# Reordering VectorE and ScalarE steps in a two-layer graph attention kernel

## The chip, the core and the metric

The kernel runs on one core of a Trainium2 chip. The metric is the device time of one execution in microseconds. Before the change it is 2905.23 us, the median of 3 runs (2905.09 to 2909.05).

A core has five engines that the text names: TensorE (PE; its weight loads are shown apart as PEld), VectorE (DVE), ScalarE (ACT), GpSimd (POOL) and SyncE (SP). Each works through its own queue of instructions, and they wait for one another by semaphores. In this kernel SP issues nearly all transfers between HBM and the core's own memory (SBUF). PSUM is the memory that TensorE writes its products to.

## The reference

Two layers run over 64 graphs of 256 nodes with 512 features each, in float32, each layer with a residual and a layer norm:

```python
# layer 0: graph attention, 8 heads of 64
feats = einsum('bnf,hfu->bhnu', X, W)
e_self, e_neigh = einsum('bhnu,hu->bhn', feats, a_self), einsum('bhnu,hu->bhn', feats, a_neigh)
dense = leaky_relu(e_self[..., :, None] + e_neigh[..., None, :], 0.2) + -1e10 * (1 - A)
out = relu(concat(softmax(dense) @ feats) + b)
x = layernorm(x + out)
# layer 1: attention with adjacency and distance (here the adjacency again) added to the softmax
q, k, v = split(x @ W_qkv)
attn = 0.33 * softmax(mask(q @ k.T / 8)) + 0.33 * adj + 0.33 * exp(-dist)
x = layernorm(x + (attn @ v) @ W_out + b_out)
```

## The kernel before

**The loop.** One graph (b) is a unit of work. The main loop (L1469) runs over b = 1 to 63 and calls two functions in turn: attention0_beside_projections1(b) (L1266), where layer 0's attention of graph b is mixed with layer 1's projections of graph b-1, and attention1_beside_projections0(b) (L1350), where layer 1's attention of graphs b-1 and b-2 is mixed with layer 0's projection of graph b+1. So four graphs are in flight. One pass of both functions is called a turn here. start() and end() hold the first and the last graphs.

**The order is written out by hand.** do(stage, b, step, ...) (L1160) emits one step and then calls in_order() (L94), which ties every new instruction to the one before it on the same engine. So each engine runs its instructions exactly in the order in which the do lines stand, and a step that is moved past another changes the order on every engine that both use.

**Products with seven instead of eight parts.** Four big products (layer 0's projection pf, q and k pq, values pv, output po) are 2 x 2 block products in the form with seven products and some sums. left_factors (L290) makes the sums of the moving side, four VectorE differences t1 to t4: t2 reads t1, t4 reads t2, and t3 stands alone. It serves xC (from x, L442), hC (from the first layer's output, L851) and oC (from layer 1's heads, in half_blocks, L1036). seven() (L309) issues the products and their combination. Its PSUM banks matter here: p1, p6, p7 and p4 accumulate in one bank ("chain"), and after each of them ScalarE copies the bank (L329) before the next may add to it. The adds (qk_add, v_add, product_add, add: L332) are on VectorE.

**What the change touches, in the order of a turn:**
- attend1 squares (L1029) and store (L1128): layer norm of a finished graph; squares on ScalarE with small steps on GpSimd, then two activations on ScalarE (L391) and the output's transfer on SP. rows_again and load_rows issue two more transfers on SP.
- proj1 qk p1, p2, p6, p5, p7 and, later, p4, p3: q and k. "The third copy" is the copy of p6, q and k's third product; it stands behind the store's two activations in ScalarE's queue.
- proj0 columns (L579): one VectorE difference nd, then two small exponentials on ScalarE (ccol, and the factor kept in V0).
- proj0 scaled(h) (L646): 2 activations for each of 8 heads on ScalarE, 16 in all; attend0 weights(h) (L680): 2 VectorE steps for each head.
- turned xC: the four differences of x for the next graph.
- attend0 product (L702): TensorE's av, 128 matmuls; rec0 (L724): two reciprocals on VectorE; norm0 (L729): 16 activations on ScalarE that read them.
- attend1 weights(g) (L979), g = 0 to 3: a VectorE product and, on its result, a VectorE sum, 128 x 1024 each.
- proj1 values: pv, seven parts; proj0 product: pf, seven parts; aT: a VectorE transpose of the adjacency.
- softmax1 scores(g) (L872): TensorE's pz, then two exponentials on ScalarE (L896), one for each half j; both(g) (L904): a VectorE pair sum; sums (L927): TensorE's row sums pd; invert (L933): VectorE's transpose, reciprocal and product with the row mask, then a ScalarE copy; inverted (L950): VectorE's transpose and two transfers.
- proj1 hT: VectorE's transpose of hb, which SP reloads from HBM.
- shared (L472): the additive part of layer 1's attention: a VectorE sum (part 0), two VectorE steps with the mask, even (L490) and a last sum (part 1).

The lines of the output's stretch, as they stand before:

```python
do("softmax1", b - 1, "scores", 2)
do("softmax1", b - 1, "scores", 3)
do("attend1", b - 2, "half_blocks", 1)
do("softmax1", b - 1, "both", 2)
do("attend1", b - 2, "product", "p1")
```

## Time and profile before

| what | before |
|---|---|
| median of 3 runs | 2905.23 us |
| the profiled execution's own time | 2909.9 us |
| its span, first to last instruction | 2908.1 us |
| mean granted TensorE clock | 0.994 |
| HBM traffic, over the span | 123 GB/s |
| one turn in the middle (1388.55 to 1432.66 us) | 44.11 us |
| in that turn: TensorE busy, its weight loads | 44.03 us, 33.94 us |
| in that turn: VectorE, ScalarE busy | 40.31 us, 27.51 us |

How to read it: the page and the answers of the trace give the busy time of an engine as the union of its instructions, so two that overlap are counted once. A line of the timeline has the start, the length, the engine, the source line, the operation, what it writes and reads, the shape and the count; in square brackets stands how long the engine had been idle and whom it waited for. A line of the waits has the time in total, the number of times and the longest. The ends of TensorE's matmuls are modelled, so stalls of TensorE are read from starts.

### The profile page before, as it was taken

Reading aid. Unit: us, or ns where it says so; the run is one execution under the profiler, and the core shown is the slowest. Engines: PE = TensorE matmul, PEld = TensorE weight load, DVE = VectorE, ACT = ScalarE, POOL = GpSimd, SP = SyncE. Lnnn points to the kernel's source line nnn. Section 1 sums busy time; section 2 is a strip of 40 time slices with the busy share of each in tenths; the row PEclk is TensorE's granted clock in tenths of the full one; section 3 lists DMA queues with packets and bytes.
Section 4 is the critical chain, followed back from the end, with each engine's and each line's share of the span. In section 5 each row is a group of like instructions: output and inputs, shape, how many; then the busy total and the mean of one; then the engine's idle time right before and its main releaser. Section 6 shows DMA issues by size and latency. Waiting matters only on the chain.

```text
span 2908.1 us, 93475 instructions
## 1 busy us (share of the span) xinstructions
PE 2867.5 (99%) x39110; PEld 2210.9 (76%) x39110; DVE 2589.3 (89%) x5147; ACT 1761.9 (61%) x4905; POOL 234.9 (8%) x526
## 2 busy tenths in 40 slices
PE   8899999999999999999999999999999999999998
PEld 7677777877777777877877877777777778778775
DVE  6799999999989989999999999999899999998984
ACT  3556666665666666666666656656666666666663
POOL 0001000000100100000000001001000000000001
PEclk8999999999999999999999999999999999999999
DMA  6345444454454454454444554554554544544432
GB/s 136 89 126 125 128 136 119 129 141 119 124 143 118 123 135 120 129 134 121 133 121 129 139 119 129 135 124 122 135 124 127 136 115 134 133 122 134 119 111 70
DMA packets 778972, 363.89 MB, mean 125 GB/s; under 512 B 694604, under 2 KB 696636, under 8 KB 762552
## 3 DMA queue, kind: packets, MB, share of 16 engines
q1 hardware_dynamic: 776440, 357.37, 47.5%
q8 instruction: 311, 5.10, 0.8%
q14 instruction: 109, 0.89, 0.1%
q10 hardware_dynamic: 2112, 0.52, 0.1%
HBM read 289.42 MB, written 68.13 MB: 123 GB/s over the span
## 4 chain that ended last, share of the span: by engine, by line
PE 77%; ACT 8%; DMA 7%; DVE 3%; SPq 2%; issue 2%; POOL 2%; ACTq 0%; DVEq 0%; POOLq 0%
PE pq_p L87 26%; PE pv_p L87 13%; PE po_p L87 10%; PE pf_p L87 9%; PE av L714 8%; ACT p L896 4%; PE pz L881 4%; PE av L998 3%; DMA hb<-hs 3%; DMA hs<-x 2%; PE pd L916 2%; SPq L122 2%; DMA gs<-grow 1%; ACT x L391 1%; ACT junk L372 1%
## 5 line engine op out<-in xcount | busy, mean ns | idle before, releaser
L87 PE MATMUL pq_p<-hC,wqk_sb 128*64 128x128 f32 x8192 | 485.3, 274 | 4.9 <-ACT qk L329 2.9
L87 PEld LDWEIGHTS pq_p<-hC,wqk_sb 128*64 128x64 f32 x8192 | 449.4, 137 | 21.0 <-ACT qk L329 20.6
L691 DVE SCALAR_TENSOR_TENSOR pT<-gb,ccol,at 128x256 f32<-128x256 f32 x992 | 403.3, 479 | 50.3 <-ACT ccol L588 50.3
L87 PE MATMUL pq_p<-hT,wqk_sb 128*64 128x128 f32 x6144 | 358.2, 273 | 0.6 <-DVE hT L129 0.5
L87 PEld LDWEIGHTS pq_p<-hT,wqk_sb 128*64 128x64 f32 x6144 | 342.4, 137 | 10.5 <-DVE hT L129 1.0
L896 ACT ACTIVATE p<-pz,hide 128x512 f32<-128x512 f32 x512 | 315.0, 682 | 30.9 <-PE pz L881 30.5
L745 ACT ACTIVATE x<-av,rec 128x64 f32<-128x64 f32 x1008 | 224.8, 366 | 155.5 <-DVE rec L727 155.5
L988 DVE TENSOR_TENSOR p<-p,ct 128x1024 f32<-128x1024 f32 x252 | 308.8, 1225 | 8.6
L981 DVE TENSOR_TENSOR p<-p,rb 128x1024 f32<-128x1024 f32 x252 | 303.7, 1205 | 5.1 <-DMA rb<-rs 5.1
L87 PE MATMUL pv_p<-wv_sb,hC 128*64 128x256 f32 x2048 | 250.5, 386 | 9.8 <-ACT v L329 9.8
L714 PE MATMUL av<-v,pT 128*64 128x65 f32 x8192 | 255.5, 223 | 2.5 <-issue 2.0
L881 PE MATMUL pz<-qk 64*128 64x256 f32 x2048 | 256.2, 389 | 1.8 <-ACT p L896 1.7
L714 PEld LDWEIGHTS av<-v,pT 128*64 128x64 f32 x8192 | 251.5, 139 | 4.9 <-issue 4.6
L87 PE MATMUL pf_p<-wf_sb,xC 128*64 128x264 f32 x1984 | 254.0, 386 | 0.1
L648 ACT ACTIVATE v<-v 128x64 f32<-128x64 f32 x1024 | 251.8, 338 | 0.0
L87 PE MATMUL po_p<-wo_sb,oC 128*64 128x256 f32 x1984 | 238.4, 382 | 4.3 <-DVE o L332 1.0
L881 PEld LDWEIGHTS pz<-qk 64*128 64x128 f32 x2048 | 187.1, 186 | 69.4 <-issue 48.9
L998 PE MATMUL av<-p,v 128*64 128x256 f32 x2016 | 228.8, 379 | 0.2 <-DVE p L988 0.2
L329 ACT COPY v<-pv_p 128x256 f32<-128x256 f32 x256 | 102.3, 399 | 196.1 <-PE pv_p L87 195.9
L87 PEld LDWEIGHTS pv_p<-wv_sb,hC 128*64 128x64 f32 x2048 | 149.5, 138 | 90.1 <-ACT v L329 26.4
L87 PEld LDWEIGHTS po_p<-wo_sb,oC 128*64 128x64 f32 x1984 | 136.9, 137 | 95.4 <-ACT o L329 31.5
L87 PEld LDWEIGHTS pf_p<-wf_sb,xC 128*64 128x64 f32 x1984 | 148.4, 137 | 71.3 <-DVE v L332 0.8
(165 smaller groups left out, 4399.7 us busy)
## 6 DMA issues: line engine op xcount, KB each, us to landing
rb<-rs SPq DMA_DIRECT2D x63, 1024.0 KB
gb<-gs SPq DMA_DIRECT2D x62, 1028.0 KB
hs<-x SPq DMA_DIRECT2D x64, 512.0 KB
xb<-in_x_dram SPq DMA_DIRECT2D x252, 128.0 KB
x<-in_x_dram SPq DMA_DIRECT2D x63, 512.0 KB
hb<-hs SPq DMA_DIRECT2D x252, 128.0 KB
y<-hs SPq DMA_DIRECT2D x63, 512.0 KB
out_dram<-y SPq DMA_DIRECT2D x63, 512.0 KB
```

Source lines behind the costliest of these rows:

```text
L87: matmul(dst[cols], lhsT[:, cols], rhs, **flags)
L122: nc.sync.dma_start(dst[q * B : (q + 1) * B], src.rearrange("(k r) (c q s) -> q r c k s", r=B, q=Q, s=B)[q],)
L329: nc.scalar.copy(out[COPIES[p]], dst)
L648: nc.scalar.activation(V0[b][:, t, h, :U], V0[b][:, t, h, :U], AF.Copy, scale=V0[b][:, t, h, U : U + 1],)
L691: nc.vector.scalar_tensor_tensor(pT[h][:, j, :], GB[b][h], CCOL[b][:, j, h : h + 1], AT[b][:, j, :], op0=ALU.max, op1=ALU.mult,)
L714: matmul(av[r * half : (r + 1) * half, k, :], pT[h][:, j, i : i + half], V0[b][:, j, h, :UA], start=(j == 0), stop=(j == T - 1),)
L745: nc.scalar.activation(X1[b][:, t, h * U : (h + 1) * U], av[:, k, :U], AF.Copy, scale=REC0[g][:, t, k : k + 1],)
L881: matmul(pz[:, r, j, :], QK[b][rows, g, 1, j * P : (j + 1) * P], QK[b][rows, g, 0, :], start=True, stop=True,)
L896: nc.scalar.activation(p[:, :, j, :], pz[:, :, j, :], AF.Exp, bias=hide[:, j, b : b + 1], scale=U**-0.5,)
L981: nc.vector.tensor_mul(p, p, REC[b][:, k : k + 2, g // 2, :] .unsqueeze(2) .to_broadcast([P, 2, T, N]),)
L988: nc.vector.tensor_add(p, p, CT[b].unsqueeze(1).to_broadcast([P, 2, T, N]))
L998: matmul(av[0][r * U : (r + 1) * U, g % 2, :], V1[b][:, j, 2 * g + r, :], PROBS[b][g][:, r, j, :], start=(j == 0), stop=(j == T - 1),)
```

## The change

No instruction is added or taken away; steps are put in another order.
- left_factors takes the list of differences to make, and makes them as t1, t3, t2, t4 by default.
- attend1 weights(g) can be made in two steps (product, then sum), and other VectorE steps stand between the two.
- x's four differences move from ahead of attend0's product to behind the two reciprocals, between the steps of weights 0 and 1.
- columns moves ahead of the second squares; q and k's p6 moves ahead of the store, rows_again and load_rows.
- aT moves between the steps of weights 2, and add 11 between those of weights 3.
- The exponentials of scores 3 are issued apart: the first stays, the second moves behind the output's p1. hT moves ahead of the last pair sum.
- The row sums move ahead of hC, and the steps of invert alternate with hC's four differences.
- even moves from shared's second part to its first.

```diff
--- before.py
+++ after.py
@@ -287,16 +287,18 @@
     k1, k2 = slice(0, C2), slice(C2, C)
     n1, n2 = slice(0, P), slice(P, N)
 
-    def left_factors(sums, hT, part=None):
+    def left_factors(sums, hT, which=(0, 2, 1, 3)):
 
         t1, t2, t3, t4 = (sums[:, i] for i in range(4))
-        if part != 1:
-            nc.vector.tensor_sub(t1, hT[:, k1, n2], hT[:, k1, n1])
-            nc.vector.tensor_sub(t2, hT[:, k2, n2], t1)
-        if part == 0:
-            return
-        nc.vector.tensor_sub(t3, hT[:, k2, n2], hT[:, k1, n2])
-        nc.vector.tensor_sub(t4, hT[:, k2, n1], t2)
+        for i in which:
+            if i == 0:
+                nc.vector.tensor_sub(t1, hT[:, k1, n2], hT[:, k1, n1])
+            elif i == 1:
+                nc.vector.tensor_sub(t2, hT[:, k2, n2], t1)
+            elif i == 2:
+                nc.vector.tensor_sub(t3, hT[:, k2, n2], hT[:, k1, n2])
+            else:
+                nc.vector.tensor_sub(t4, hT[:, k2, n1], t2)
 
 
 
@@ -474,6 +477,10 @@
             if part != 1:
                 CT[b] = work.tile([P, T, N], FT, tag="ct", name=f"ct_{b}", bufs=3)
                 nc.vector.tensor_add(CT[b], pa, FAR[0])
+                FAR[2] = work.tile([P, N], FT, tag="far", name=f"even_{b}", bufs=1)
+                nc.vector.tensor_scalar(
+                    FAR[2], mrow, -LA / N, LA / N, op0=ALU.mult, op1=ALU.add
+                )
             if part == 0:
                 return
             for j in range(T):
@@ -485,13 +492,8 @@
                     op0=ALU.mult,
                     op1=ALU.mult,
                 )
-
-            even = work.tile([P, N], FT, tag="far", name=f"even_{b}", bufs=1)
-            nc.vector.tensor_scalar(
-                even, mrow, -LA / N, LA / N, op0=ALU.mult, op1=ALU.add
-            )
             nc.vector.tensor_add(
-                CT[b], CT[b], even.unsqueeze(1).to_broadcast([P, T, N])
+                CT[b], CT[b], FAR[2].unsqueeze(1).to_broadcast([P, T, N])
             )
 
         def from_rows():
@@ -871,8 +873,8 @@
 
         def scores(g, part=None):
 
-            if part == 1:
-                exponentials(g, PZ.pop(g), range(T))
+            if part:
+                exponentials(g, PZ[g], range(T) if part == 1 else (part - 2,))
                 return
             pz = psum.tile([P, 2, T, N], FT, tag="sc", name=f"pz_{b}_{g}", bufs=2)
             for j in range(T):
@@ -930,22 +932,27 @@
                 sums(pd, g)
             PD[0] = pd
 
-        def invert():
+        def invert(step=None):
 
             K = 2 * N // B
-            zd = work.tile([P, K, B], FT, tag="far", name=f"zd_{b}", bufs=1)
-            nc.vector.transpose(
-                zd.rearrange("p k s -> p (k s)"), PD[0].rearrange("p g n -> p (g n)")
-            )
-            inv = small.tile([P, K], FT, tag="inv", name=f"inv_{b}", bufs=2)
-            nc.vector.reciprocal(inv, zd[:, :, 0])
+            if step in (None, 0):
+                zd = PD["blocks"] = work.tile([P, K, B], FT, tag="far", name=f"zd_{b}", bufs=1)
+                nc.vector.transpose(
+                    zd.rearrange("p k s -> p (k s)"), PD[0].rearrange("p g n -> p (g n)")
+                )
+            zd = PD["blocks"]
+            if step in (None, 1):
+                inv = PD["inv"] = small.tile([P, K], FT, tag="inv", name=f"inv_{b}", bufs=2)
+                nc.vector.reciprocal(inv, zd[:, :, 0])
+            if step in (0, 1):
+                return
+            inv = PD["inv"]
             nc.vector.tensor_mul(
                 inv.rearrange("p (g i) -> p g i", g=2),
                 inv.rearrange("p (g i) -> p g i", g=2),
                 rowmask[:, b // B, :, b % B].unsqueeze(1).to_broadcast([P, 2, N // B]),
             )
             nc.scalar.copy(zd, inv.unsqueeze(2).to_broadcast([P, K, B]))
-            PD["blocks"] = zd
 
         def inverted():
             zd = PD["blocks"]
@@ -976,15 +983,18 @@
             oT = work.tile([P, C, N], FT, tag="xC", name=f"oT_{b}", bufs=1)
         av = {}
 
-        def weights(g):
+        def weights(g, step=None):
             p, k = PROBS[b][g], 2 * (g % 2)
-            nc.vector.tensor_mul(
-                p,
-                p,
-                REC[b][:, k : k + 2, g // 2, :]
-                .unsqueeze(2)
-                .to_broadcast([P, 2, T, N]),
-            )
+            if step != 1:
+                nc.vector.tensor_mul(
+                    p,
+                    p,
+                    REC[b][:, k : k + 2, g // 2, :]
+                    .unsqueeze(2)
+                    .to_broadcast([P, 2, T, N]),
+                )
+            if step == 0:
+                return
             nc.vector.tensor_add(
                 p, p, CT[b].unsqueeze(1).to_broadcast([P, 2, T, N])
             )
@@ -1035,10 +1045,10 @@
 
         def half_blocks(part):
             if part == 1:
-                left_factors(SEVEN["sums"], oT, 1)
+                left_factors(SEVEN["sums"], oT, (3,))
                 return
             SEVEN["sums"] = oC = work.tile([P, 4, C2, P], FT, tag="xC", name=f"oC_{b}", bufs=1)
-            left_factors(oC, oT, 0)
+            left_factors(oC, oT, (0, 2, 1))
             SEVEN["o"] = o = io.tile([P, T, F], FT, tag="xb", name=f"o_{b}", bufs=1)
             SEVEN["product"], SEVEN["add"] = seven_rows(
                 f"po_{b}",
@@ -1269,13 +1279,13 @@
         if b > 1:
             do("attend1", b - 4, "squares", slice(0, 1), False)
             do("proj1", b - 1, "qk", "p1")
+            do("proj0", b, "columns")
             do("attend1", b - 4, "squares", slice(1, 2), slice(0, 2))
             do("proj1", b - 1, "qk", "p2")
-            do("proj0", b, "columns")
+            do("proj1", b - 1, "qk", "p6")
             do("attend1", b - 4, "store")
             do("attend1", b - 3, "rows_again")
             load_rows(b)
-            do("proj1", b - 1, "qk", "p6")
             for h in range(HG):
                 do("proj0", b, "scaled", h)
                 do("attend0", b, "weights", h)
@@ -1287,14 +1297,18 @@
                 do("attend0", b, "weights", h)
             do("proj1", b - 1, "qk", "p7")
             do("proj1", b - 1, "qk_add", 22)
-            if b + 1 < NB:
-                do("turned", b + 1, "xC")
         for g in range(2):
             for t in range(T):
                 do("attend0", b, "product", g, t)
         do("attend0", b, "rec0", 0)
         do("attend0", b, "rec0", 1)
-        do("attend1", b - 2, "weights", 0)
+        turned = 1 < b < NB - 1
+        do("attend1", b - 2, "weights", 0, 0)
+        if turned:
+            do("turned", b + 1, "xC", (0, 2))
+        do("attend1", b - 2, "weights", 0, 1)
+        if turned:
+            do("turned", b + 1, "xC", (1,))
         if b == 1:
             do("proj0", b, "shared")
             load_rowmask()
@@ -1309,7 +1323,10 @@
             do("attend0", b, "norm0", 1, t)
         if b > 1:
             do("proj1", b - 1, "qk", "p3")
-        do("attend1", b - 2, "weights", 1)
+        do("attend1", b - 2, "weights", 1, 0)
+        if turned:
+            do("turned", b + 1, "xC", (3,))
+        do("attend1", b - 2, "weights", 1, 1)
         if b > 1:
             do("proj1", b - 1, "qk_add", 12)
         do("attend0", b, "end")
@@ -1327,13 +1344,14 @@
             load(b + 2)
         do("proj0", b + 1, "product", "p1")
         do("proj1", b - 1, "values", "p4")
-        do("attend1", b - 2, "weights", 2)
+        do("attend1", b - 2, "weights", 2, 0)
         do("attend0", b, "squares", slice(0, 1), False)
         do("proj0", b + 1, "product", "p6")
         do("attend0", b, "squares", slice(1, 2), slice(0, 2))
         do("proj1", b - 1, "values", "p3")
+        do("proj0", b + 1, "aT")
+        do("attend1", b - 2, "weights", 2, 1)
         do("proj1", b - 1, "v_add", 12)
-        do("proj0", b + 1, "aT")
         do("proj0", b + 1, "product", "p5")
         do("proj0", b + 1, "product", "p7")
         do("attend0", b, "norm")
@@ -1343,8 +1361,9 @@
         do("proj0", b + 1, "product", "p4")
         do("proj0", b + 1, "far")
         do("proj0", b + 1, "product", "p3")
-        do("attend1", b - 2, "weights", 3)
+        do("attend1", b - 2, "weights", 3, 0)
         do("proj0", b + 1, "add", 11)
+        do("attend1", b - 2, "weights", 3, 1)
         do("proj0", b + 1, "add", 12)
 
     def attention1_beside_projections0(b):
@@ -1368,21 +1387,28 @@
             do("attend1", b - 2, "values", g)
         do("attend1", b - 2, "half_blocks", 0)
         do("softmax1", b - 1, "scores", 2)
-        do("softmax1", b - 1, "scores", 3)
+        do("softmax1", b - 1, "scores", 3, 0)
+        do("softmax1", b - 1, "scores", 3, 2)
         do("attend1", b - 2, "half_blocks", 1)
         do("softmax1", b - 1, "both", 2)
         do("attend1", b - 2, "product", "p1")
+        do("softmax1", b - 1, "scores", 3, 3)
+        do("proj1", b, "hT")
         do("softmax1", b - 1, "both", 3)
         do("attend1", b - 2, "product", "p2")
-        do("proj1", b, "hT")
         do("attend1", b - 2, "product_add", 11)
         do("attend1", b - 2, "product", "p6")
         do("attend1", b - 2, "product", "p5")
         do("attend1", b - 2, "product", "p7")
         do("attend1", b - 2, "product_add", 22)
-        do("proj1", b, "hC")
         do("softmax1", b - 1, "sums")
-        do("softmax1", b - 1, "invert")
+        do("proj1", b, "hC", (0,))
+        do("softmax1", b - 1, "invert", 0)
+        do("proj1", b, "hC", (2,))
+        do("softmax1", b - 1, "invert", 1)
+        do("proj1", b, "hC", (1,))
+        do("softmax1", b - 1, "invert", 2)
+        do("proj1", b, "hC", (3,))
         do("attend1", b - 2, "product", "p4")
         do("proj0", b + 1, "bias")
         do("softmax1", b - 1, "inverted")
```

In the diff as shown, the hunks that only pass arguments on are left out: sums of turned makes its tile once and hands on the list, and hC does the same.

More of the change, by code (lines that the diff above doesn't have):

```diff
@@ L440, in transposes, with sums @@
             transpose_blocks(XT[b], XB[b])
-        def sums():
-            XC[b] = work.tile([P, 4, C2, P], FT, tag="xC", name=f"xC_{b}", bufs=1)
-            left_factors(XC[b], XT[b])
+        def sums(which=(0, 2, 1, 3)):
+            if b not in XC:
+                XC[b] = work.tile([P, 4, C2, P], FT, tag="xC", name=f"xC_{b}", bufs=1)
+            left_factors(XC[b], XT[b], which)
         return dict(xT=transposes, xC=sums)
@@ L850, in proj1 @@
             from_rows=from_rows,
-            hC=lambda: left_factors(hC, hT),
+            hC=lambda *which: left_factors(hC, hT, *which),
             blocks=rows_to_blocks,
```

## The prediction

> **What bounds the kernel now.** I read first the busy shares, then the waits by engine, then the timeline of one turn of the main loop in the middle of the run. The first line names the engine.
>
> ```profile
> PE 2867.5 (99%) x39110; PEld 2210.9 (76%) x39110; DVE 2589.3 (89%) x5147; ACT 1761.9 (61%) x4905; POOL 234.9 (8%) x526
> ```
>
> TensorE's ends are modelled, so 99% doesn't say that it never stalls; its weight loads, at 76%, show the stalls. The waits of PEld (us in total, times, longest) name three that depend on another engine:
>
> ```profile
> PEld po_p L87 <- ACT o L329: 31.5, 62, 1.0
> PEld pv_p L87 <- ACT v L329: 28.6, 54, 7.5
> ...
> PEld pq_p L87 <- ACT qk L329: 20.6, 65, 1.1
> ```
>
> All three are a product of seven() that reuses the "chain" bank and has to wait until ScalarE has copied the product before it. No wait for VectorE comes above 2.2 us in total. So VectorE, at 89%, isn't what holds TensorE, and the shorter VectorE chains by themselves bring nothing. The timeline of one turn (start, us, engine, line) shows what ScalarE was doing instead of the copy:
>
> ```profile
> 1401.27 1.96 PE L87 MATMUL pq_p<-hC,wqk_sb 128*64 128x128 f32 x32
> ...
> 1404.77 1.93 PE L87 MATMUL pv_p<-wv_sb,hT 128*64 128x256 f32 x16
> ...
> 1406.53 2.81 PE L87 MATMUL pv_p<-wv_sb,hC 128*64 128x256 f32 x24
> ...
> 1424.40 2.42 ACT L896 ACTIVATE p<-pz,hide 128x512 f32<-128x512 f32 x4 [0.48 <-PE pz L881]
> ...
> 1425.15 1.95 PE L87 MATMUL po_p<-wo_sb,oT 128*64 128x256 f32 x16
> ...
> 1426.70 0.39 ACT L329 COPY o<-po_p 128x256 f32<-128x256 f32 x1
> ...
> 1427.14 2.81 PE L87 MATMUL po_p<-wo_sb,oC 128*64 128x256 f32 x24
> ...
> 1432.66 3.66 PE L87 MATMUL pq_p<-hT,wqk_sb 128*64 128x128 f32 x64
> ...
> 1436.15 5.67 PE L87 MATMUL pq_p<-hC,wqk_sb 128*64 128x128 f32 x96
> ...
> 1437.81 1.52 ACT L391 ACTIVATE y<-y,shift_l,rstd_l 128x512 f32<-128x512 f32 x2 [1.28 <-POOL shift_l L387]
> 1439.23 0.56 ACT L329 COPY qk<-pq_p 128x512 f32<-128x512 f32 x1
> 1439.70 3.93 ACT L648 ACTIVATE v<-v 128x64 f32<-128x64 f32 x16
> ...
> 1441.64 3.90 PE L714 MATMUL av<-v,pT 128*64 128x65 f32 x128
> ...
> 1446.20 0.28 DVE L727 RECIPROCAL rec<-av 128x8 f32<-128x8 f32 x2
> ...
> 1446.43 1.75 ACT L745 ACTIVATE x<-av,rec 128x64 f32<-128x64 f32 x8 [2.34 <-DVE rec L727]
> ```
>
> A turn is 44.11 us (1388.55 to 1432.66, pq_p to pq_p). Steps without a stall: 64 pq_p in 1436.15 - 1432.66 = 3.49, so 0.0545 each; 8 pv_p from 1410.06 to 1410.92, so 0.108 each; 128 av from 1441.64 to 1445.38 (the next pq_p), so 0.0292 each. Against these, the stalls:
> - po_p: 16 in 1.99 us instead of 1.73. About 0.05 of that follows the change from the scores' tile shape, so 0.21 is the wait; the first pair after a wait is another 0.05 late. 0.26 us.
> - pq_p: 96 in 5.49 instead of 5.23. 0.26 us.
> - pv_p: 16 in 1.76 instead of 1.73, then 24 in 2.63 instead of 2.59. 0.07 us.
>
> Together 0.59 us of a turn. The sampled turn has PEld waits of 0.50 (po_p) and 0.28 (pq_p) where the means are 31.5/62 = 0.51 and 20.6/65 = 0.32, so it is typical and slightly kind; I use 0.62.
>
> **What the Trainium skill says.** "Perfetto Trace Analysis", Matmuls, wants matmul groups to rotate through PSUM banks so that evacuation overlaps the next group; the chain bank breaks this, and the trace agrees: only its reuses wait. The same page, under Tensor Engine Instruction, says that ScalarE and VectorE are strict FIFO and that a matmul's end is estimated; the copy at 1439.23 behind two y activations agrees. "VectorE: DVE Perf Modes", The DRAIN you can't avoid, says that the pipeline empties after each operation and that a semaphore between chained ones costs nothing extra. This trace differs: x's first difference (1400.63) to the dependent second (1401.08) is 0.45 us, the second to the independent third (1401.43) 0.35. So a dependent handover costs 0.10 us, and the measurement decides.
>
> **The change part by part.** No TensorE instruction moves against another; only when the others serve it.
>
> *Last exponential behind the output's first copy.* po_p's first product starts at 1425.15, is 8 matmuls (0.91 with the slow first pair), and ScalarE sees a product about 0.22 after its last step (the pf_p products end their steps at 1414.45, the copy starts at 1414.67): ready at 1426.28. Three exponentials at 0.58 apart free ScalarE at about 1426.15. The copy runs 1426.28 to 1426.67; TensorE wants the bank at 1426.92. Stall gone: -0.26 us. The exponential moves to about 1426.6 to 1427.3. The last pair sum waits for it, but that sum now stands behind hT's transpose (1.24 us) and starts near 1427.7; the row sums on TensorE need it at 1429.6. Covered by 1.2 us. hT is transposed about 1 us earlier than 1427.46, so it may wait for hb's load in some turns; VectorE's idle 1.24 us before the output's second add covers that.
>
> *q and k's third copy ahead of the store.* In us after pq_p's start: p6 ends its steps at 5.23, is ready at 5.45, copied by 6.02; p7 wants the bank at 6.98. Stall gone: -0.26. Behind it the store's two activations (5.92), then the 16 scalings of v, at 5.92 + 1.42 = 7.34 (was 1439.70 - 1432.66 = 7.04). These feed av, which now starts at 160 x 0.0545 = 8.72, not 8.98. The eighth head's value is ready at 7.34 + 3.93 + about 0.05 = 11.32; av reaches it after 88 matmuls at 8.72 + 2.57 = 11.29. The fourth head just fits (9.41 against 9.42). So a new wait of 0.03 and its late first pair, +0.08 to +0.10. From both sides: 0 if my chain is 0.05 too late, +0.3 if ScalarE is 0.2 later than worked out. I take +0.09. p7's copy then comes 0.3 later; p4 wants that bank at 12.46 and it is free at 11.8. SP's queue is passed in the same order (output store, y's reload, x's load), all about 0.8 us later. x is read at 1407.63 + 44.11 = 1451.74, 8 us after its issue at 1443.71; VectorE has waited for it 2 times, 0.9 us. Price 0 to +0.05 per turn, I take 0.
>
> *Reciprocals ahead of x's differences.* Before, the reciprocals start 0.82 after av's last step (1445.38), behind the four differences. Now they start at about +0.22, and ScalarE's scaling of av by +0.45 instead of +1.05. The first pv_p copy needs 3.64 us of ScalarE work before it (1402.33 to 1405.97), so ScalarE is free at +4.1; the product is ready at 3.49 + 0.86 + 0.22 = +4.57 and its bank wanted at +5.22. Stall gone: -0.07. The price is on VectorE: the differences used to fill the wait for av, and now come after it. Steps from there to q and k's last add: 0.10 + 1.12 + 0.34 + 0.34 + 1.14 + 0.34 + 1.12 + 0.34 + 1.14 = 5.98 us, so it starts at +6.2, was +5.76 (1407.03 - 1401.27). VectorE is 0.43 late and has no idle time until 1419.3. The third and fourth weights give back 0.2 (two handovers). So V0's last add (1418.28 to 1418.70) ends about 0.25 late, and the row matmuls that read it start at 1419.15: covered with 0.2 to spare, +0.02 on average.
>
> *The rest* (weights split, products' differences reordered, even moved up, invert interleaved, the columns' exponentials earlier): ten handovers or so, 1.0 us of VectorE a turn, beside TensorE's work: 0. They are what pays for the lateness just counted.
>
> Sum: -0.62 + 0.09 + 0.02 = -0.51 us a turn, over 62 turns -32 us. The profiled execution took 2909.9 us (span 2908.1), 4.7 above the median of 2905.23. Off the median: 2874 us, 1.1% less.
>
> **Rivals.**
> 1. Forecast: stalls gone, small wait at av. 2874 (2866 to 2882). 0.58.
> 2. The store's stall is traded, not removed: scalings arrive 0.3 late at av (as long as the stall that they replace), or VectorE's 0.43 is not covered at the row matmuls. For it: both margins are under 0.1 to 0.2. Against: the row matmuls waited for that add only 3 times before (1.2 us). Gain 0.51 - 0.22 = 0.29 x 62 = 18: 2887 (2882 to 2898). 0.19.
> 3. More than counted: av doesn't wait and the irregular turns (some 5 us over 44.11 in all) even out: 0.62 x 62 + 2 = 40: 2865 (2856 to 2866). 0.12.
> 4. Slower: the scalings of v, behind both the third copy and the store, hold av. Each 0.1 us beyond my 7.34 costs 6 us; from 7.9 on (0.55 later) the change loses, at 8.1 it gives 2905 + 12 = 2917. For: ScalarE is one FIFO, and every instruction between 5.4 and 11.3 is now in line without a gap. Against: before, ScalarE idled 1.28 us ahead of the store, and that gap now holds the copy. 0.08.
> 5. It doesn't do what it says: the order on ScalarE comes out as before because p1's and p6's copies wait for something else too. No change, 2905. 0.03.
>
> **How the numbers follow.** A run of this kernel can tell 0.2% (5.8 us) from no change. Faster by more: cases 1 to 3, 0.89; within: 0.03; slower: 0.08. Cases 1 and 3 and the nearer half of 2 make 8 in 10: 2860 to 2889.
>
> **What would show it.** Right: the three PEld waits for ScalarE nearly vanish, the turn is 43.6 us, the reciprocals start within 0.3 us of av's last step, TensorE's instructions stay in order. The store part wrong: a line PEld or PE av L714 <- ACT v L648 of over 10 us. Lateness uncovered: PEld pr L509 <- DVE v L332 above 5 us. The forecast falls if the three waits go and the turn doesn't shorten.

## The result and the profile after

| | before | after |
|---|---|---|
| median (4 runs each) | 2905.39 us (2905.09 to 2909.05) | 2869.66 us (2867.75 to 2870.97) |
| span of the profiled execution | 2908.1 us | 2868.8 us |
| mean granted TensorE clock | 0.994 | 0.994 |
| a turn in the middle (median) | 44.11 us | 43.50 us |

The ratio is 0.9874, with a 95% interval of 0.9857 to 0.9891: 35.7 us less, where 31 were forecast. 62 turns at 0.61 us less would be 37.8 us.

The page of the changed kernel, first its busy line of the engines, then the chain of work that ended last, by engine:

```profile
PE 2835.4 (99%) x39110; PEld 2221.5 (77%) x39110; DVE 2547.6 (89%) x5147; ACT 1793.8 (63%) x4905; POOL 248.8 (9%) x526
...
PE 96%; DVE 1%; DMA 1%; ACT 1%; SPq 0%; issue 0%; POOL 0%; DVEq 0%; POOLq 0%
```

The busy shares say almost nothing: TensorE had 99% before and has 99% now. The chain shows the difference. Before, it left TensorE for nearly a quarter of the span:

```profile
PE 77%; ACT 8%; DMA 7%; DVE 3%; SPq 2%; issue 2%; POOL 2%; ACTq 0%; DVEq 0%; POOLq 0%
```

The waits of the weight loads after the change (us in total, times, longest):

```profile
PEld pr L511 <- DVE v L334: 18.9, 57, 0.3
PEld pv_p L87 <- ACT v L331: 12.4, 4, 7.5
...
PEld pq_p L87 <- ACT qk L331: 2.8, 4, 0.9
...
PEld po_p L87 <- ACT o L331: 0.4, 1, 0.4
```

The three waits on ScalarE's copies happened 62, 65 and 54 times and now 1, 4 and 4 times; those left are in the first two turns, in the last turn and behind the loop. A new line, pr on VectorE, has 18.9 us; what it is worth is told further down.

The timeline of one turn, in the order of the lines shown before:

```profile
1401.46 0.47 PEld L511 LDWEIGHTS pr<-ident,v 128*43 128x43 f32 x8 [0.33 <-DVE v L334]
...
1407.45 1.95 PE L87 MATMUL po_p<-wo_sb,oT 128*64 128x256 f32 x16
...
1408.59 0.37 ACT L331 COPY o<-po_p 128x256 f32<-128x256 f32 x1
1408.86 0.69 ACT L898 ACTIVATE p<-pz,hide 128x512 f32<-128x512 f32 x1
...
1409.23 2.76 PE L87 MATMUL po_p<-wo_sb,oC 128*64 128x256 f32 x24
...
1414.70 3.66 PE L87 MATMUL pq_p<-hT,wqk_sb 128*64 128x128 f32 x64
...
1418.19 5.41 PE L87 MATMUL pq_p<-hC,wqk_sb 128*64 128x128 f32 x96
...
1420.16 0.59 ACT L331 COPY qk<-pq_p 128x512 f32<-128x512 f32 x1 [1.87 <-PE pq_p L87]
1420.64 1.52 ACT L393 ACTIVATE y<-y,shift_l,rstd_l 128x512 f32<-128x512 f32 x2
...
1422.06 3.92 ACT L650 ACTIVATE v<-v 128x64 f32<-128x64 f32 x16
...
1423.43 3.90 PE L716 MATMUL av<-v,pT 128*64 128x65 f32 x128
...
1427.09 0.50 DVE L729 RECIPROCAL rec<-av 128x8 f32<-128x8 f32 x2
...
1427.33 1.75 ACT L747 ACTIVATE x<-av,rec 128x64 f32<-128x64 f32 x8 [0.87 <-DVE rec L729]
```

Starts are what to read. From po_p's first product to its second kind 1.78 us (was 1.99); from pq_p's second kind to av 5.24 (was 5.49); x's scaling of av begins 3.90 us after av's start (was 4.79). In medians over 40 turns, from the start of one stage on TensorE to the next:

| stage | before | after |
|---|---|---|
| pq_p on hC (96 matmuls) | 5.49 | 5.24 |
| pv_p on hT, then on hC | 1.76 + 2.64 | 1.73 + 2.59 |
| po_p on oT, then on oC | 1.99 + 2.74 | 1.78 + 2.69 |
| av | 3.73 | 3.73 |

All other stages are equal to 0.01 us. The differences are 0.25, 0.08 and 0.26 us, together 0.59 of the 0.61.

### The profile page after: what moved, and what is told of

The parts are those of the page before. It is cut to its first block, busy times and chain, and to the rows that moved or that the text cites. A ratio compares the mean times of both kernels' runs of the same rounds, so it can differ in the third digit from the quotient of the medians.

```text
span 2868.8 us, 93413 instructions
## 1 busy us (share of the span) xinstructions
PE 2835.4 (99%) x39110; PEld 2221.5 (77%) x39110; DVE 2547.6 (89%) x5147; ACT 1793.8 (63%) x4905; POOL 248.8 (9%) x526
## 4 chain that ended last, share of the span: by engine, by line
PE 96%; DVE 1%; DMA 1%; ACT 1%; SPq 0%; issue 0%; POOL 0%; DVEq 0%; POOLq 0%
PE pq_p L87 27%; PE po_p L87 13%; PE pf_p L87 13%; PE pv_p L87 13%; PE av L716 8%; PE pz L883 8%; PE av L1008 7%; PE pd L918 2%; PE pr L511 1%; PE po L87 0%; PE pg L577 0%; DMA hb<-hs 0%; PE pf L87 0%; SPq L122 0%; DMA rb<-rs 0%
## 5 line engine op out<-in xcount | busy, mean ns | idle before, releaser
L87 PE MATMUL pq_p<-hC,wqk_sb 128*64 128x128 f32 x8192 | 472.8, 273 | 1.9 <-ACT qk L331 1.7
L898 ACT ACTIVATE p<-pz,hide 128x512 f32<-128x512 f32 x512 | 322.2, 682 | 30.2 <-PE pz L883 29.9
L331 ACT COPY qk<-pq_p 128x512 f32<-128x512 f32 x256 | 149.0, 582 | 153.4 <-PE pq_p L87 150.5
L334 DVE TENSOR_TENSOR qk<-pq_p,qk 128x512 f32<-128x512 f32 x192 | 131.6, 686 | 124.0 <-ACT qk L331 122.0
L331 ACT COPY v<-pv_p 128x256 f32<-128x256 f32 x256 | 95.7, 374 | 224.5 <-PE pv_p L87 224.3
```

The costliest lines, as they stand in the source:

```text
L87: matmul(dst[cols], lhsT[:, cols], rhs, **flags)
L331: nc.scalar.copy(out[COPIES[p]], dst)
L334: nc.vector.tensor_add(out[i], banks[ADDED[i]], out[i])
L898: nc.scalar.activation(p[:, :, j, :], pz[:, :, j, :], AF.Exp, bias=hide[:, j, b : b + 1], scale=U**-0.5,)
```

## The experiments

All kernels below are compared with the kernel before on the same chip; its medians there were 2903.98 to 2904.87 us. Positions are medians over 40 turns, in us after pq_p's start.

| kernel | median us | ratio and interval | turn |
|---|---|---|---|
| the exponential's move alone | 2888.59 | 0.9947 (0.9930 to 0.9963) | 43.82 |
| the store's move alone | 2920.11 | 1.0058 (1.0043 to 1.0073) | 44.40 |
| the reciprocals' move alone | 2926.76 | 1.0079 (1.0064 to 1.0094) | 44.49 |
| all three moves, no interleaving | 2895.52 | 0.9972 (0.9960 to 0.9983) | 43.98 |
| all interleavings, no move | 2885.25 | 0.9931 (0.9916 to 0.9946) | 43.77 |
| the inversion's interleaving alone | 2886.31 | 0.9931 (0.9914 to 0.9947) | 43.77 |
| after, third copy behind the store again | 2895.47 | 0.9963 (0.9949 to 0.9977) | 43.97 |
| after, that and the columns put back | 2868.23 | 0.9878 (0.9863 to 0.9893) | 43.50 |
| after, weights 2 and 3 not interleaved | 2874.90 | 0.9894 (0.9879 to 0.9908) | 43.60 |
| after, one spare copy ahead of the scalings | 2874.15 | 0.9891 (0.9876 to 0.9905) | 43.62 |
| after, three spare copies there | 2910.53 | 1.0026 (1.0016 to 1.0037) | 44.17 |
| after, first and last graphs reordered | 2862.69 | 0.9856 (0.9842 to 0.9871) | 43.50 |

### Each move alone

The first asks whether the output's stall goes by the exponential alone. The kernel before, with this edit (the lines of scores that let the two exponentials be issued apart are left out):

```diff
-        do("softmax1", b - 1, "scores", 3)
+        do("softmax1", b - 1, "scores", 3, 0)
+        do("softmax1", b - 1, "scores", 3, 2)
...
         do("attend1", b - 2, "product", "p1")
+        do("softmax1", b - 1, "scores", 3, 3)
```

> The kernel before with one edit: the last exponential of scores 3 stands behind the output's first copy. Theory A (three separate ScalarE stalls, each worth its own length): po_p's wait goes, the turn shrinks by 0.26 us, the time by 0.26 x 62 = 16 us, to about 2889; the pq_p and pv_p waits stay at 20 and 28 us. Theory B (the gain comes from VectorE's shorter chains): no gain here, 2905. Theory C (the stalls are coupled, one that goes comes back at the next reuse of a bank): under 8 us, and the pq_p or pv_p waits grow.

It did: po_p's stages became 1.78 and 2.69, all others stayed within 0.02, and the time fell by 16 us.

The second moves q and k's third copy alone:

```diff
+            do("proj1", b - 1, "qk", "p6")
             do("attend1", b - 4, "store")
             do("attend1", b - 3, "rows_again")
             load_rows(b)
-            do("proj1", b - 1, "qk", "p6")
```

> The kernel before with one edit: q and k's p6 stands ahead of the store and the two loads. Theory A: pq_p's wait goes, 0.26 x 62 = 16 us less, about 2889, with the scalings of v starting at 7.35 us after pq_p and no or a tiny wait at av. Theory B: 2905. Theory C: the stall is traded for one at av (the scalings arrive 0.3 us later), 2900 to 2910, and av L714 gets a wait for ACT v.

It became slower. pq_p's stage is 5.24 as expected, but pv_p's first stage went from 1.76 to 2.31. The timeline of this kernel, and its line in the waits:

```profile
1403.83 0.56 ACT L329 COPY qk<-pq_p 128x512 f32<-128x512 f32 x1
1404.42 0.69 DVE L332 TENSOR_TENSOR qk<-pq_p,qk 128x512 f32<-128x512 f32 x1 [0.97 <-ACT qk L329]
...
1406.49 0.28 DVE L727 RECIPROCAL rec<-av 128x8 f32<-128x8 f32 x2
...
1406.73 1.74 ACT L745 ACTIVATE x<-av,rec 128x64 f32<-128x64 f32 x8 [2.34 <-DVE rec L727]
...
1410.36 0.50 ACT L329 COPY v<-pv_p 128x256 f32<-128x256 f32 x1
...
1410.91 2.81 PE L87 MATMUL pv_p<-wv_sb,hC 128*64 128x256 f32 x24 [0.41 <-ACT v L329]
```

```profile
PEld pv_p L87 <- ACT v L329: 62.8, 63, 7.5
```

Read downwards: p7's copy, at 11.19 instead of 10.88, holds VectorE's add of q and k; the add holds x's differences and the reciprocals (13.85 instead of 13.55); these hold ScalarE's scaling of av, and that holds the copy which TensorE needs (17.72 instead of 17.43). TensorE arrives there 0.25 us earlier and the copy 0.29 later, on a wait that had no slack: 0.54 of the 0.55.

The third moves x's differences behind the reciprocals alone, all four together:

```diff
-            if b + 1 < NB:
-                do("turned", b + 1, "xC")
...
         do("attend0", b, "rec0", 1)
+        if 1 < b < NB - 1:
+            do("turned", b + 1, "xC")
```

> The kernel before with one edit: the two reciprocals ahead of x's four differences, which then follow in one piece; no weights are split. Theory A: pv_p's small stall goes (0.07 us a turn), but VectorE reaches V0's last add about 0.75 us late, where only some 0.4 us are free before the row matmuls: a new stall of 0.3 to 0.4 us a turn at pr, so slower by 14 to 20 us, 2919 to 2925. Theory B and a careless reading of A (a stall goes, nothing is late): 2901.

Slower, as the second reading had it. The first of the two reciprocals comes at 12.08 instead of 13.55 and the pv_p wait is gone. In its place the waits show (us, times, longest):

```profile
PEld pf_p L87 <- DVE v L332: 36.7, 60, 0.6
...
PEld pr L509 <- DVE v L332: 26.0, 60, 0.4
```

The larger loss isn't at the row matmuls pr (the stage ahead of them went from 1.93 to 2.03) but earlier, where pf's last product waits for VectorE's add 22 of layer 0's projection: the add ends at 27.87 and the product starts at 27.92 (the stage ahead of that product went from 1.78 to 2.11, its own from 0.99 to 1.04).

All three moves together (with hT's and the columns'), without any interleaving; that is the changed kernel with left_factors, weights, aT, add 11, hC, invert and even in the old order:

> The changed kernel with its three moves, but every VectorE interleaving undone: differences in the order t1, t2, t3, t4 and in one piece, weights in one piece, aT and add 11 at their old places, invert in one piece behind hC, even back in its old place. Theory A: the interleavings bring nothing by themselves but pay for VectorE's lateness; without them V0's last add is late as in the run with the reciprocals alone, so 0.3 to 0.4 us a turn come back: 2870 + 19 to 25 = 2889 to 2895. If interleavings were free of any effect: 2870. Theory B (they are the main gain): near 2905.

All three stalls of the forecast are gone, and both new ones of the third experiment are there: pf_p 34.6 us in 57 waits, and the same stages 2.11, 1.04 and 2.03. From this kernel to the changed one the interleavings take off 26 us, or 0.48 us of a turn, which is what these three stages had gained in length.

### The interleavings

The changed kernel with its three moves, hT's and the columns' undone, so that x's four differences are ahead of av again:

> The changed kernel with its moves undone (store ahead of p6, columns behind squares, both exponentials of scores 3 together, hT behind p2, x's differences ahead of av), and all VectorE interleavings kept. As the prediction has it, they bring nothing by themselves: 2905. Theory A, read again after the first four runs: invert's interleaving hands ScalarE its work some 0.7 us earlier, so the squares, GpSimd's small steps and the store end about 0.4 us earlier; p6's copy then ends at about 6.75 us after pq_p where p7 wants the bank at 6.98, and pq_p's stall of 0.26 us goes without the store's move; with the reciprocals a little earlier pv_p's 0.07 goes too; po_p's 0.26 stays. 44.11 - 0.33 = 43.78 us a turn, 2885.

20 us came off where the prediction had 0. pq_p's stage is 5.24 and pv_p's stages 1.73 and 2.59 without any move; the output's stall is still there (1.99). Which interleaving does it? The kernel before, with the inversion's alone:

```diff
-        do("proj1", b, "hC")
         do("softmax1", b - 1, "sums")
-        do("softmax1", b - 1, "invert")
+        do("proj1", b, "hC", (0,))
+        do("softmax1", b - 1, "invert", 0)
+        do("proj1", b, "hC", (2,))
+        do("softmax1", b - 1, "invert", 1)
+        do("proj1", b, "hC", (1,))
+        do("softmax1", b - 1, "invert", 2)
+        do("proj1", b, "hC", (3,))
```

> The kernel before with one of the interleavings alone: the differences of h between the steps of the inversion. With all interleavings and no move the store began 4.97 us after pq_p's start instead of 5.15, and pq_p's stage fell from 5.49 to 5.24 us. If that comes from the inversion (ScalarE's copy of the inverted sums heads its line and waits for VectorE, and everything up to the store stands behind it), this kernel has a pq_p stage of 5.24 to 5.3 and a time of 2885 to 2891; the values' stage may lose its 0.07 us as well. If the other interleavings carry it, pq_p's stage stays at 5.49 and the time at 2902 to 2906.

(The 4.97 in it was misread: the store begins at 4.76 in both kernels.) This one does all of it: turn and stages equal those of the run with all interleavings. The timeline of the kernel before shows where it comes from:

```profile
1430.74 0.41 DVE L294 TENSOR_TENSOR hC<-hT 128x256 f32<-128x256 f32 x1
...
1431.87 0.42 DVE L299 TENSOR_TENSOR hC<-hT,hC 128x256 f32<-128x256 f32 x1
1432.20 0.71 DVE L937 STREAM_TRANSPOSE zd<-pd 128x512 f32<-128x512 f32 x1
...
1433.24 0.19 DVE L942 TENSOR_TENSOR inv<-inv,rowmask 128x16 f32<-128x16 f32 x1
...
1433.52 0.62 ACT L947 COPY zd<-inv 128x512 f32<-128x512 f32 x1 [3.15 <-DVE inv L942]
1434.04 0.36 ACT L329 COPY o<-po_p 128x256 f32<-128x256 f32 x1
1434.30 0.72 ACT L372 ACTIVATE junk<-y,nmean_l 128x512 bf16<-128x512 f32 x1
...
1437.81 1.52 ACT L391 ACTIVATE y<-y,shift_l,rstd_l 128x512 f32<-128x512 f32 x2 [1.28 <-POOL shift_l L387]
1439.23 0.56 ACT L329 COPY qk<-pq_p 128x512 f32<-128x512 f32 x1
```

And the same stretch with the inversion's interleaving alone:

```profile
1420.22 0.41 DVE L296 TENSOR_TENSOR hC<-hT 128x256 f32<-128x256 f32 x1
...
1420.55 0.71 DVE L949 STREAM_TRANSPOSE zd<-pd 128x512 f32<-128x512 f32 x1
...
1421.93 0.17 DVE L959 TENSOR_TENSOR inv<-inv,rowmask 128x16 f32<-128x16 f32 x1
1422.04 0.42 DVE L302 TENSOR_TENSOR hC<-hT,hC 128x256 f32<-128x256 f32 x1
...
1422.14 3.66 PE L87 MATMUL pq_p<-hT,wqk_sb 128*64 128x128 f32 x64
1422.19 0.62 ACT L964 COPY zd<-inv 128x512 f32<-128x512 f32 x1 [2.34 <-DVE inv L959]
...
1422.71 0.37 ACT L340 COPY o<-po_p 128x256 f32<-128x256 f32 x1
1422.98 0.72 ACT L383 ACTIVATE junk<-y,nmean_l 128x512 bf16<-128x512 f32 x1
...
1426.90 1.52 ACT L402 ACTIVATE y<-y,shift_l,rstd_l 128x512 f32<-128x512 f32 x2 [1.28 <-POOL shift_l L398]
1428.33 0.56 ACT L340 COPY qk<-pq_p 128x512 f32<-128x512 f32 x1
```

ScalarE's copy of the inverted sums heads its line and waits for VectorE. It starts at 0.85 before and at 0.05 here. Of these 0.80 us the first squares get all, but p1's copy only 0.40 (2.36 to 1.96), since there it meets TensorE's end of p1; the store then begins at 4.76 instead of 5.15, and the third copy is done at 6.75, ahead of the 6.98 at which p7 wants the bank. The reciprocals and pv_p's copy come 0.39 earlier too. ScalarE's queue wasn't reordered for that.

VectorE's was, and two things are in its 0.79 us. From hC's first difference to the inversion's last step it took 2.50 us before (1430.74 to 1433.24) and takes 1.71 here. The fourth difference, one step of some 0.34 us, now stands behind that last step instead of ahead of it. The other 0.45 or so goes with the alternation: before, three of the seven steps read what the step just before them had written, now none does, and from the first of them to VectorE's next instruction it takes 2.16 us instead of 2.60. No run separates the two. An estimate from the lines above: the fourth difference alone, moved behind, would have the third copy done at about 6.8 (7.14 before, less 0.34), and that is also ahead of 6.98. So what is shown is that the earlier inversion removes the stall, not that it has to be interleaved.

### The edits around the store, in company

The changed kernel with only the third copy back behind the store:

```diff
-            do("proj1", b - 1, "qk", "p6")
             do("attend1", b - 4, "store")
             do("attend1", b - 3, "rows_again")
             load_rows(b)
+            do("proj1", b - 1, "qk", "p6")
```

> The changed kernel with p6 put back behind the store and the loads, everything else kept. If the store's move carries the 0.26 us of pq_p's stall, as the prediction has it: 43.50 + 0.26 = 43.76 us a turn, 2870 + 16 = 2886. Theory A read again: the interleaved invert and the earlier columns let the store end early enough for p6's copy, so 2870, the same within 4 us, and the scalings of v start about 0.4 to 0.7 us earlier than with the move.

Both guesses missed: pq_p's stage is 5.71, worse than before the change, and the waits have this line:

```profile
PEld pq_p L87 <- ACT qk L331: 31.9, 64, 0.9
```

The reason is the columns, which in this kernel still stand ahead of the second squares. Their two exponentials push these to 2.79 (2.45 with the inversion's interleaving alone), and the store begins at 5.36, not 4.76; the third copy behind it ends at 7.35, after 6.98. GpSimd, whose small steps stand between the squares and the store, has a part in it: the first of them starts 0.33 us later and takes 0.47 us instead of 0.19. So one edit (columns) delays the store by 0.6 us, and another (third copy) repairs it. With both put back:

```diff
-            do("proj0", b, "columns")
             do("attend1", b - 4, "squares", slice(1, 2), slice(0, 2))
             do("proj1", b - 1, "qk", "p2")
-            do("proj1", b - 1, "qk", "p6")
+            do("proj0", b, "columns")
             do("attend1", b - 4, "store")
             do("attend1", b - 3, "rows_again")
             load_rows(b)
+            do("proj1", b - 1, "qk", "p6")
```

> The changed kernel with the whole of its edit on ScalarE's queue around the store undone: the columns' exponentials again behind the second squares, the store again ahead of q and k's third copy. The exponential's move, the reciprocals' move and the interleavings stay. If the store's stall went because the interleaved inversion brings the squares and with them the store forward, and the move was not needed, pq_p's stage stays at 5.24 us, the turn at 43.50 and the time at 2867 to 2872. If the move itself removed the stall, as the prediction has it, pq_p's stage is 5.5 us and the time about 2886.

The time and all stages are those of the changed kernel. The store's move isn't needed beside the interleaved inversion, and this version has more room: v's scalings begin at 6.65 instead of 7.36.

### The two margins

VectorE's, at layer 0's last add. The changed kernel with the steps of weights 2 and 3 together again, aT and add 11 behind them as before:

```diff
-        do("attend1", b - 2, "weights", 2, 0)
+        do("attend1", b - 2, "weights", 2)
...
-        do("proj0", b + 1, "aT")
-        do("attend1", b - 2, "weights", 2, 1)
         do("proj1", b - 1, "v_add", 12)
+        do("proj0", b + 1, "aT")
...
-        do("attend1", b - 2, "weights", 3, 0)
+        do("attend1", b - 2, "weights", 3)
         do("proj0", b + 1, "add", 11)
-        do("attend1", b - 2, "weights", 3, 1)
```

> The changed kernel with only weights 2 and weights 3 in one piece again (aT behind v's last add, add 11 behind weights 3). VectorE loses two dependent handovers of 0.10 us between the reciprocals and V0's last add. If VectorE's margin there is what the trace says (add 22 ends 0.24 us before pf_p's p3 starts, V0's last add 0.21 before pr): pf_p doesn't wait yet, pr at most 0.1 us a turn, so 2870 to 2876. If any lateness is paid at once: 0.2 x 62 = 12, 2882.

As expected: 0.10 us of a turn, at pr. ScalarE's, ahead of av, with n spare copies (of a tile that nothing reads):

```diff
             load_rows(b)
+            for _ in range(n):
+                spare = small.tile([P, F], BF, tag="junk", name="spare", bufs=1)
+                nc.scalar.copy(spare[:, :U], bo_bc[:, :U])
+                in_order()
             for h in range(HG):
                 do("proj0", b, "scaled", h)
```

> The changed kernel with one more ScalarE copy (128 x 64, a step of about 0.24 us, its result unused) between the store and the scalings of v. The trace has the eighth head's scaling end at 1425.98 and av reach it at 1426.0: no margin. If so, av waits 0.22 us and its late first pair 0.05: +0.24 to 0.29 us a turn, 2885 to 2888. If there is a margin of 0.2 us or more that the trace doesn't show: 2870.

A miss in its size: the copy moved the scalings by 0.14 us only (7.36 to 7.50), and av's stage grew by 0.12 (3.73 to 3.85). Both the prediction and this expectation took the eighth head's value to be needed whole after 88 of av's matmuls. But product (L702) reads a head's two halves one after the other, two matmuls each, and so needs the second half, the one scaled last, only after 92. In the changed kernel that scaling ends at 11.28 and av reads it at 11.41; for the fourth head it is 9.37 and 9.55. So there is a slack of about 0.1 us. One spare copy uses it up: av waits some 0.02 us at the fourth head, and there and at the eighth the next pair of matmuls starts 0.10 to 0.11 us behind the one before instead of 0.06. With n = 3:

> The changed kernel with three small ScalarE copies of an unused tile ahead of the scalings of v. One such copy moved the scalings by 0.14 us and av's stage from 3.73 to 3.85 us. If ScalarE's line ahead of av is the limit from about 0.05 us of delay on, as rival 4 has it (each 0.1 us costs 6 us), three copies move the scalings by 0.14 + 2 x 0.24 = 0.6 us, av's stage becomes about 4.3 us, the turn about 44.05 and the time 2900 to 2908, so that the whole gain is gone. If something behind av absorbs the delay, the time stays below 2890.

The scalings begin at 8.05, av's stage is 4.39, and the whole gain is gone: 40.9 us for 0.69 us of delay. In this run the waits hardly show it; besides "issue" these are their lines for av of layer 0:

```profile
PEld av L716 <- ACT qk L331: 0.2, 1, 0.2
PEld av L716 <- ACT v L650: 0.2, 1, 0.2
```

The 0.66 us of a turn are spread over eleven pairs of matmuls, which start 0.10 to 0.13 us behind the pair before instead of 0.06. Ten of them stand in a row (9.16 to 10.23), and every second of these starts about 0.05 us after a scaling of v has ended (9.16 after 9.11, 9.40 after 9.35). The list has none of these short waits.

### The first and the last graphs

After the change the long stalls of TensorE lie outside the loop's steady part. The edit is aimed at four of them: 7.4 us at 75, 2.0 at 2801, 1.0 at 2814 and 2.9 at 2830. The largest: pv_p's third product waits for a copy behind x's scaling in ScalarE's line, and its reciprocals stand on VectorE behind the transpose of the next x and the difference of weights. The main edit puts these behind the reciprocals (the line that keeps the later p1 for the other turns is left out):

```diff
-        do("turned", 2, "xT")
-        do("turned", 2, "xC")
-        right_factors(wf_sb, wf12)
-        in_order()
...
         do("attend0", b, "rec0", 1)
+        if b == 1:
+            do("proj1", 0, "values", "p1")
+            do("turned", 2, "xT")
+            do("turned", 2, "xC")
+            right_factors(wf_sb, wf12)
+            in_order()
```

In the last turn the fourth pair sum goes ahead of hT, and behind the loop two third copies go forward (only the new places are shown):

```diff
+        do("proj1", b, "qk", "p2")
+        do("proj1", b, "qk", "p6")
         do("attend1", b - 3, "store")
...
         do("attend1", b - 1, "values", 3)
+        do("proj1", b, "values", "p6")
         do("softmax1", b, "scores", 2)
```

> The changed kernel with the main loop left as it is and its ends reordered: in the first turn the reciprocals and the first product of values ahead of the next x's transposes and the difference of weights; in the last turn the fourth pair sum ahead of hT's transpose, which waits for its load; after the loop q and k's third copy ahead of the store, and the values' third copy ahead of the last four exponentials. The stalls of TensorE there in the changed kernel are 7.4 us at 75, 2.0 at 2801, 0.96 at 2814 and 2.9 at 2830. If they are stalls of order and no other wait stands right behind them, some 6 to 12 us go and the time is 2858 to 2864; if other waits take their place, it stays within 3 us of 2869.7.

Its median is 7 us below that of the changed kernel; the intervals of the two ratios overlap, so the trace must say what is real. The timeline of its first turn:

```profile
75.46 1.90 PE L87 MATMUL pv_p<-wv_sb,hC 128*64 128x256 f32 x16
...
78.79 1.08 PE L87 MATMUL pv_p<-wv_sb,hC 128*64 128x256 f32 x8 [1.43 <-ACT v L331]
...
83.95 1.08 PE L87 MATMUL pv_p<-wv_sb,hC 128*64 128x256 f32 x8 [1.44 <-DVE v L334]
```

The long stall is gone; from start to start two of 1.8 us stand there now, one for the copy behind x's scaling, one for VectorE. From the last stall ahead of this stretch (pq_p at 65) to the first behind it (pz at 98) the changed kernel takes 32.81 us and this one 27.22: 5.6 us gained. Counted from TensorE's first matmul, the part behind the loop begins 6.35 us earlier, but TensorE's last matmul only 5.0: there the stall of 2.9 us moved from the values' p7 to their p4 (3.3), behind the same four exponentials. So the start is worth its reordering; that of the end gave nothing, and of the 7 us of the medians the trace accounts for 5.

## Why the prediction was right, and where it wasn't

**The bound and the sum: right.** TensorE bound by three reuses of the chain bank, 0.59 us of a turn; these are the stages that became shorter, by 0.59. VectorE's busy share wasn't the limit: its time fell only from 2589 to 2548 us, and no stage that became shorter had waited for it directly. The order of its steps did matter, as told below.

**The exponential: right.** -0.26 forecast, -0.26 in its stages, -0.29 of the turn alone; the pair sum behind hT cost nothing.

**"Stall gone: -0.26" for the third copy: it is gone, but the move is neither enough nor needed.** "p7's copy then comes 0.3 later; p4 wants that bank at 12.46 and it is free at 11.8" looked at the bank alone. VectorE's add stands behind that copy, and the reciprocals behind the add; alone, the move costs 16 us. With the reciprocals no longer behind x's differences this doesn't happen (pv_p's stages are 1.73 and 2.59 with all three moves). And with the inversion's interleaving the stall goes without the move.

**+0.09 for av: the mis-sized term.** Scalings were forecast at 7.34 and av at 8.72; they came at 7.36 and 8.73, and av waited 0. The times were right; the count of matmuls wasn't. The last half of a head is read four matmuls later than the prediction has it, 4 x 0.029 = 0.12 us, and that is the cover which it missed. The price of rival 4, 6 us for each 0.1 us, is what the three spare copies measured (40.9 us for 0.69), and its place too: a delay to 8.05 is slower than before. Without the 0.09 the forecast moves towards the rival in which av doesn't wait (2865), and the result lies between the two.

**The reciprocals: right in what they free, wrong in where they cost.** The first comes at 12.39, while av's last matmuls run, and pv_p's wait is gone, as it is with this move alone. But the inversion's interleaving alone removes it too, with the reciprocals at 13.16; whether the changed kernel needs this move wasn't tried. The lateness of VectorE was looked for at pr; it is felt first at pf's last product (0.33 us in the run of this move alone), which the prediction doesn't name. In the changed kernel add 22 ends at 1398.30 and the product starts at 1398.54; layer 0's last add ends at 1401.25 and pr starts at 1401.46. So both places hold by about 0.2 us.

**The 0 for "the rest" is the step that failed.** The interleavings were costed at nothing since the list of waits has TensorE hardly waiting for VectorE. It did wait, at one remove: the inversion's last step held ScalarE's line, and so the store and the third copy, and the list names only ScalarE, the last in the row. Alone this is worth 18 to 20 us, and beside the moves the interleavings are worth 26, there by keeping VectorE early enough for pf and pr, as the prediction said ("what pays for the lateness"). The columns, also in that 0, cost the store 0.6 us, which the third copy's move then repairs. That the total came out right all the same is in part luck: these omissions cancel, because a stall can go only once and the moves need a cover that the interleavings give. The single edits (16 and 20 us gained, 16 and 22 lost) sum to a loss of some 3 us; together they give 36.

**The signs.** The three waits and the turn came as described. Two other signs were badly chosen. A wait of pr for VectorE above 5 us was to show lateness; it is 18.9 us, and costs nothing: the same 0.3 us stood there before as "issue" (19.6 us in 59), where the matmuls' tile shape changes, and the stage ahead of pr is 1.93 in both. And a wait of av above 10 us wouldn't have shown even the 41 us of three spare copies.

Which of the smaller interleavings (weights 0 and 1, even, oC's differences) adds what wasn't tried apart, nor was a kernel with the exponential's move and the inversion alone; the single gains of these two, 16 and 18 us, would sum to nearly all.

## What to carry to other kernels

Follow a late instruction through the queues of both engines, not only to the buffer that it frees: a ScalarE copy delayed by 0.3 us came back six steps later at another stall. When an engine's line begins with an instruction that waits for another engine, bring that chain forward first; here this removed, with ScalarE's queue as it was, a stall for which that queue had been reordered. Count what a consumer reads first and last: it may need the last piece later than the first. Judge edits of one order together and by stage lengths from start to start, since a stall that one edit removes can't be removed by another. And look at starts when a list of waits shows nothing: the waits of under 0.1 us each, 41 us together, didn't appear in it here.

## What the runs showed of the hardware

- GpSimd's step of two elements a partition (rstd) took 0.19 us where it started just ahead of VectorE's first pT step (all interleavings, no move: 3.34 and 3.40), and 0.47 us in the changed kernel, where it started while pT steps ran (1418.37, pT running since 1417.51). What in it depends on VectorE wasn't taken apart.
- At pr, where the matmuls' tile shape changes, a wait of 0.33 us for VectorE (18.9 us in 57) cost nothing: a gap of 0.33 us stood there before without one (19.6 us in 59). A wait of 0.42 us (24.9 us in 59, weights 2 and 3 not interleaved) cost 0.10.
- A ScalarE copy of 128 x 64 lasted 0.23 to 0.25 us. Three to the same tile started 0.26 and 0.28 us apart, but the first scaling of v started only 0.15 us after the last of them, so one copy moved the scalings by 0.14 and three by 0.69.
- After a wait the next pair of TensorE's matmuls starts late as well: 0.11 us behind the first instead of 0.06 (av with one spare copy, 9.57 to 9.68), about 0.05 us on top of the wait.
